# Local attention in a four-stage kernel: another written order of its steps

## The chip, the core and the metric

The kernel runs on one core of a Trainium2 chip. TensorE (PE) multiplies matrices, and loads its weights beside that (PEld); VectorE (DVE), ScalarE (ACT) and GpSimd (POOL) compute elementwise and reduce; SyncE (SP) issues DMAs. Each engine works through its own instructions in the order in which they were written and waits for the others by semaphores. The metric is the device time of one execution in microseconds (us), shown as the median of several runs. The profile comes from one further execution.

## The reference

The program has four stages over 16 sequences of 256 tokens and 128 features: a full attention, a transformer of six layers with local attention, a state space model and a small feed-forward layer. The change lies in the second stage, which computes this for each layer (shortened):

```python
qkv = x @ Wqkv                                  # 16 heads of 64
q, k = l2norm(q) * qs, l2norm(k) * ksc
q = q * cos * scale + rotate_half(q) * sin * scale
k = k * cos * inv + rotate_half(k) * sin * inv
sim = einsum('bhwie,bhwje->bhwij', bq, bk2) * 8  # windows of 32, look back one window
attn = softmax(where(mask, -max, sim), -1)
x = einsum('bhwij,bhwje->bhwie', attn, bv2) @ Wo + x
x = (a * gelu(gate)) @ W2 + b2 + x               # a, gate from the normalized x
```

Before both halves of a layer, half of the features are shifted by one token (shift_tokens).

## The kernel before

Everything is float32. In the transformer the 16 sequences form 8 groups of two, so that six layers give 48 groups. A group's work is cut into named steps, each of which is a method of the class Transformer. In a step's name, q or k says which of the two is made, the first digit is the sequence in the group (b), the second the half of 128 tokens (t), and a third, where there is one, a half of the data.

PE's steps are P (L613, projection of q or k, two matmuls of 512 columns), T (L687, 16 transposes of 64 rows), X (L714, two transposes of the input), S (L744, 64 small score matmuls), G (L802, eight matmuls that apply the probabilities, in four row groups of 32 side by side), Y (L823, four heads of the output projection, four Ys for each sequence), and, in the feed-forward half, F1 (L843), F5, FP (L899) and FY (L923).

DVE's steps are C and N (L629, L641, rotary products), R (L653, sums of squares), RR, MX and SB (L757, L763, maximum and its subtraction), SM (L776), TP (L790, transpose of the probabilities), FADD, F2, FM (L910) and FF. FF adds the layer's result to the state F; in the last layer it issues four instructions more. ACT's are Q (L623, squares), E (L704, copies of T's result to qT or kT), W (L717, copy of X's result), K (L731, the mask into the score tile), EX (L772, exponentials), B (L813, copies of G's result to `at`), SQ, F4, F6 and FE. POOL's are A (L660), M (L675), NR (L783), MXS, F3 and FN. V is two DMAs on SP's queue, which make the copy of W's result that is shifted by one window.

The order is written out by hand as a list of 172 steps, ORDER. The text behind the @ of a step is its lag. In period p the loop walks through the list once and issues each step for group p minus its lag, so one period interleaves steps of up to four groups:

```python
for p in range(n + last):
    ...
    if j >= NG - 2 and i + 1 < DEPTH:
        self.value_output(i + 1, j - NG + 2)
    ...
    for name, lag in steps:
        if 0 <= p - lag < n:
            self.step(name, groups[p - lag])
```

In the last two periods of the first five layers, value_output (L593, L603) makes half of the next layer's product of value and output weights, ahead of the period's first step: 8 small matmuls into a tile pw and two ACT copies out of it. In the fifth period of a layer, load fetches the next layer's weights.

PE writes to PSUM, where the steps share five tiles: three of the kind `two` (two banks each: pq of P, pt of T, s of K and S, pa of G, fp of FP, pw) and two of the kind `one`. They are handed out by a list of free ones, in the order of the program:

```python
def take(self, shape, name, uses=1):
    i = self.free.pop(0)
```

A step that takes a tile waits until the last reader of that tile's user before has finished. A pq is dropped after Q, C and N have read it, an s after SB, an fp after FE and FM. G takes two tiles of the kind `two`, each with half of the windows, and drops nothing but its input; the B steps drop them:

```python
for i in range(2):
    g.pa[b, t, i] = self.two.take([P, 2, HEADS * W], "pa")
```

Of the kernel before, what the change touches and what calls it, by code (L numbers as in the profile page):

```python
# [34 lines left out]
FF = int(D * 4 * 2 / 3)  # L35
# [423 lines left out]


ORDER = """
Pq00@0 FM2@3 Cq00@0 Nq000@0 EX01@1 Mq10@1 Mk10@1 SM01@1 EX00@1 G10@2 Qq000@0 FADD0@2 B101@2 B100@2
Ak11@1 FY@3 Nq001@0 Aq00@0 SM00@1 Qq001@0 Rq00@0 G11@2 B111@2 FF@3 Mq11@1 X0@1 Pk01@0 Ck01@0 Tk10@1
B110@2 Pq01@0 Nk010@0 Nk011@0 W0@1 Ek10@1 Qk010@0 Cq01@0 Qk011@0 Pk00@0 Ak01@0 Tq10@1 V0@1 Qk000@0
Qk001@0 Nq010@0 Nq011@0 Aq01@0 NR00@1 Y10@2 Eq10@1 Y11@2 Qq010@0 Qq011@0 Rk01@0 Rk00@0 NR01@1 Ck00@0
K10@1 Nk000@0 Rq01@0 MXS0@0 Mk11@1 Tq11@1 Eq11@1 S10@1 Nk001@0 TP00@1 Ak00@0 Pq11@0 MX10@1 SB10@1
SQ0@0 Qq110@0 Nq110@0 Nq111@0 Cq11@0 Pq10@0 Qq100@0 Qq101@0 Tk11@1 Y12@2 Qq111@0 Nq100@0 Nq101@0
Cq10@0 Ek11@1 Y13@2 FADD1@2 G00@1 K11@1 B000@1 S11@1 TP01@1 B001@1 X1@1 G01@1 RR0@0 EX10@1 Aq10@0
MX11@1 Mk00@0 SB11@1 F1@2 F2@2 B010@1 B011@1 Mq00@0 W1@1 EX11@1 Rq10@0 Mq01@0 Pk10@0 Pk11@0 Qk110@0
Tk00@0 Ek00@0 F3@2 FN@2 F4@2 Ck10@0 Nk100@0 Nk101@0 Ck11@0 Aq11@0 V1@1 Y00@1 Tq00@0 Eq00@0 Y01@1  # L470
Tq01@0 F5@2 Qk100@0 Y02@1 Qk101@0 K00@0 SM11@1 F6@2 Mk01@0 SM10@1 S00@0 Eq01@0 Tk01@0 Rk10@0 Nk110@0
Nk111@0 NR11@1 TP11@1 Qk111@0 MX00@0 SB00@0 Ek01@0 FP0@2 FE0@2 Rk11@0 K01@0 FP1@2 NR10@1 Y03@1
Rq11@0 MXS1@0 FE1@2 FM0@2 FM1@2 Ak10@0 SQ1@0 TP10@1 RR1@0 S01@0 MX01@0 FP2@2 FE2@2 SB01@0
"""


# [1106 lines left out]
```

## Time and profile before

| what | value |
|---|---|
| median of 3 runs | 3877.59 us (3875.69 to 3879.16) |
| profiled execution | 3872.05 us, its span 3870.2 us |
| first P of the transformer | 431.4 us after the span's start |
| last FF | ends at 3321.3 us, with its four last additions at 3323.3 us |
| mean granted TensorE clock | 0.985 |

The first 430 us of the span are the full attention, the stretch to 3323 us is the transformer, and the rest are the other two stages. From one group's F1 to the next group's there are 47 distances, of which the last two, at the end, are shorter because steps of earlier lags have run out.

A row of the page's section on slices has one digit for each fortieth of the span, in tenths of busy time. A row of the windows view gives the window, its length, and the busy time and number of instructions of PE, PEld, DVE, ACT and POOL, then the granted clock, the DMA share and GB/s. A row of the timeline gives start, duration, engine, line, operation, tiles written and read, shapes, number of merged instructions, and in brackets the idle time before and what ended it. A row of the waits view tells who waited for whom: us in total, times, the longest. Matmuls are pipelined and their ends are modelled, so the distance from one step's start to the next one's is what PE spends on it.

### The profile page before, as it was taken

What the parts mean: (1) busy time and instruction counts of PE and PEld (TensorE: products, weight loads), DVE (VectorE), ACT (ScalarE), POOL (GpSimd) and SP (SyncE); (2) the same over time, 40 slices, a digit from 0 to 9 for tenths busy, and PEclk for the clock granted to TensorE, in tenths of its full rate; (3) what the DMA queues carried; (4) which work ended last, traced back from release to release, by engine and by line L of the source; (5) the groups of instructions that cost most, each with busy time, mean ns of one, the idle gap of its engine ahead of it and who ended that gap; (6) DMA issues with size and microseconds to landing.
All of it is one profiled execution on the core that took longest, in us unless ns stands there. A gap on an engine that the chain in (4) does not pass through costs nothing. (4 is left out here: it accounts for less than half of the span.)

```text
span 3870.2 us, 104028 instructions
## 1 busy us (share of the span) xinstructions
PE 3691.9 (95%) x45040; PEld 2197.4 (57%) x45040; DVE 3386.8 (88%) x4736; ACT 2820.3 (73%) x4008; POOL 2604.4 (67%) x1636
## 2 busy tenths in 40 slices
PE   8999689999999999999999999999999999699997
PEld 4445355665656656655655656666566556355554
DVE  4665489999999999999999999999999998399997
ACT  3565467777777777777777777777777676589895
POOL 2222477777777777777777777777777775288887
PEclk9999799999999999999999999999999999899999
DMA  1000001000010000100001000000000000243432
GB/s 54 8 7 5 1 7 34 6 7 6 6 35 6 6 7 6 34 6 7 6 5 34 7 6 6 15 25 6 6 7 6 6 6 7 65 111 103 128 108 71
DMA packets 84166, 94.42 MB, mean 24 GB/s; under 512 B 8873, under 2 KB 55805, under 8 KB 82941
## 3 DMA queue, kind: packets, MB, share of 16 engines
q1 hardware_dynamic: 83708, 87.76, 8.3%
q8 instruction: 355, 5.82, 0.7%
q14 instruction: 103, 0.84, 0.1%
HBM read 73.84 MB, written 2.62 MB: 20 GB/s over the span
## 5 line engine op out<-in xcount | busy, mean ns | idle before, releaser
L660 POOL TENSOR_TENSOR u<-u,w 128x1024 f32<-128x1024 f32 x384 | 907.7, 2368 | 402.3 <-DVE w L641 236.7
L675 POOL TENSOR_TENSOR u<-u,r 128x1024 f32<-128x1024 f32 x384 | 725.0, 1904 | 17.6 <-DVE r L671 14.9
L823 PE MATMUL py<-at,wvo 128*128 128x256 f32 x3072 | 733.2, 387 | 3.7 <-ACT at L813 2.3
L613 PE MATMUL pq<-wqk,F 128*128 128x512 f32 x1536 | 715.3, 603 | 9.8 <-ACT sq L623 3.3
L623 ACT ACTIVATE sq<-pq 128x512 f32<-128x512 f32 x768 | 432.8, 600 | 300.1 <-PE pq L613 155.1
L823 PEld LDWEIGHTS py<-at,wvo 128*128 128x128 f32 x3072 | 566.5, 191 | 105.7 <-issue 22.5
L641 DVE TENSOR_TENSOR w<-pq,sinl 128x512 f32<-128x512 f32 x768 | 499.6, 681 | 8.9 <-ACT sq L623 2.1
L629 DVE TENSOR_TENSOR u<-pq,cosl 128x1024 f32<-128x1024 f32 x384 | 466.8, 1216 | 45.6 <-PE pq L613 42.5
L813 ACT COPY at<-pa 128x1024 f32<-128x1024 f32 x384 | 368.7, 1012 | 157.4 <-PE pa L802 157.4
L653 DVE TENSOR_REDUCE ss<-sq 128x16 f32<-128x1024 f32 x384 | 451.7, 1197 | 6.2 <-ACT sq L623 6.2
L613 PEld LDWEIGHTS pq<-wqk,F 128*128 128x128 f32 x1536 | 276.7, 191 | 296.6 <-issue 256.3
L802 PE MATMUL pa<-pT,xw 32*128 32x512 f32 x3072 | 407.0, 616 | 5.2 <-ACT sq L623 1.8
L783 POOL TENSOR_TENSOR pp<-pp,sm 128x1024 f32<-128x1024 f32 x192 | 363.7, 1915 | 32.0 <-DVE sm L779 32.0
L687 PEld LDWEIGHTS pt<-ident,u 64*128 64x128 f32 x6144 | 224.9, 140 | 228.1 <-issue 77.2
L1324 DVE TENSOR_TENSOR_SCAN s<-da,db 128x512 f32<-128x512 f32 x256 | 301.1, 1208 | 24.6 <-PE db L1318 12.7
L744 PEld LDWEIGHTS s<-kT,qT 64*32 64x32 f32 x24576 | 255.9, 105 | 88.3 <-issue 79.0
L687 PE MATMUL pt<-ident,u 64*128 64x64 f32 x6144 | 276.7, 230 | 30.4 <-ACT sq L623 10.9
L744 PE MATMUL s<-kT,qT 64*32 64x64 f32 x24576 | 288.8, 227 | 15.3 <-issue 10.4
L757 DVE TENSOR_REDUCE mx<-s 128x16 f32<-128x1024 f32 x192 | 230.4, 1200 | 66.4 <-PE s L744 64.8
L252 DVE TENSOR_REDUCE mx<-s 128x2 f32<-128x512 f32 x256 | 165.3, 687 | 139.9 <-PE sT L280 121.5
L802 PEld LDWEIGHTS pa<-pT,xw 32*128 32x128 f32 x3072 | 179.9, 185 | 170.2 <-issue 75.9
L899 PE MATMUL fp<-hT,w 128*128 128x512 f32 (+1 forms) x576 | 273.2, 611 | 0.9 <-ACT hT L884 0.9
(212 smaller groups left out, 6275.7 us busy)
## 6 DMA issues: line engine op xcount, KB each, us to landing
btd<-bc SPq DMA_DIRECT2D x72, 512.0 KB
bte<-bc SPq DMA_DIRECT2D x56, 256.0 KB
xw<-xw SPq DMA_DIRECT2D x96, 96.0 KB
wqk<-in_Wqk SPq DMA_DIRECT2D x6, 1024.0 KB
wv<-in_LWvT SPq DMA_DIRECT2D x6, 512.0 KB
wo<-in_Wo SPq DMA_DIRECT2D x6, 512.0 KB
xin<-in_x SPq DMA_DIRECT2D x8, 256.0 KB
out<-ot SPq DMA_DIRECT2D x8, 256.0 KB
```

Of the source, the lines that this page charges most:

```text
L613: nc.tensor.matmul(q.p[:, x], self.F[:, g.b0 + b, o : o + P], g.l.wqk[:, k, x, :], start=True, stop=True)
L623: self.c.nc.scalar.activation(q.sq[:, x], q.p[:, x], AF.Square)
L629: self.c.nc.vector.tensor_tensor(q.u.rearrange("p h x d -> p x h d"), q.p, g.l.cosl[:, t, k].unsqueeze(2).to_broadcast([P, 2, HEADS, DH // ...
L641: self.c.nc.vector.tensor_tensor(q.w[:, :, x], q.p[:, 1 - x], g.l.sinl[:, t, k, x, :].unsqueeze(1).to_broadcast([P, HEADS, DH // 2]), ALU. ...
L653: self.c.nc.vector.tensor_reduce(g.ss[b][:, t, k, :], q.sq.rearrange("p x h d -> p h x d"), AX.XY, ALU.add)
L660: self.c.nc.gpsimd.tensor_tensor(q.u, q.u, q.w, ALU.add)
L675: self.c.nc.gpsimd.tensor_tensor(uf, uf, g.r[b][:, t, k, :].unsqueeze(2).to_broadcast([P, HEADS, DH]), ALU.mult)
L687: self.c.nc.tensor.matmul(q.pt[:, r, j, :], uf[rs, j * P : (j + 1) * P], self.c.ident[rs, rs], is_transpose=True, start=(j == 0), stop=Tru ...
L744: nc.tensor.matmul(s[qs, e, j, :], qT[es, j, qs], kT[es, j, ks : ks + 2 * W], start=False, stop=True, skip_group_check=True,)
L802: self.c.nc.tensor.matmul(g.pa[b, t, w // 2][:, w % 2, :], self.xw[b][qs, t, k, :], g.pT[b, t][qs, k, :], start=(k == 0), stop=(k == 1),)
L813: self.c.nc.scalar.copy(self.at[:, :, o : o + 2 * W].rearrange("p h (w q) -> p w h q", q=W), g.pa[b, t, i].rearrange("p w (h q) -> p w h q ...
L823: self.c.nc.tensor.matmul(g.py[b], g.l.wvo[:, h, :], self.at[:, h, :], start=(h == 0), stop=(h == HEADS - 1),)
```

## The change

The list ORDER is replaced by another order of the same 172 steps. No step, tile, size or engine is changed. 25 steps change their lag: Tq00, Tk00, Tk01, S00, S01, with their E, K, MX and SB, and Mk01, Ak10, MXS1, SQ1 and RR1 go from lag 0 to 1; Y02, Y03, W1, V1 and TP11 from 1 to 2; FM0 from 2 to 3.

```diff
 ORDER = """
-Pq00@0 FM2@3 Cq00@0 Nq000@0 EX01@1 Mq10@1 Mk10@1 SM01@1 EX00@1 G10@2 Qq000@0 FADD0@2 B101@2 B100@2
-Ak11@1 FY@3 Nq001@0 Aq00@0 SM00@1 Qq001@0 Rq00@0 G11@2 B111@2 FF@3 Mq11@1 X0@1 Pk01@0 Ck01@0 Tk10@1
-B110@2 Pq01@0 Nk010@0 Nk011@0 W0@1 Ek10@1 Qk010@0 Cq01@0 Qk011@0 Pk00@0 Ak01@0 Tq10@1 V0@1 Qk000@0
-Qk001@0 Nq010@0 Nq011@0 Aq01@0 NR00@1 Y10@2 Eq10@1 Y11@2 Qq010@0 Qq011@0 Rk01@0 Rk00@0 NR01@1 Ck00@0
-K10@1 Nk000@0 Rq01@0 MXS0@0 Mk11@1 Tq11@1 Eq11@1 S10@1 Nk001@0 TP00@1 Ak00@0 Pq11@0 MX10@1 SB10@1
-SQ0@0 Qq110@0 Nq110@0 Nq111@0 Cq11@0 Pq10@0 Qq100@0 Qq101@0 Tk11@1 Y12@2 Qq111@0 Nq100@0 Nq101@0
-Cq10@0 Ek11@1 Y13@2 FADD1@2 G00@1 K11@1 B000@1 S11@1 TP01@1 B001@1 X1@1 G01@1 RR0@0 EX10@1 Aq10@0
-MX11@1 Mk00@0 SB11@1 F1@2 F2@2 B010@1 B011@1 Mq00@0 W1@1 EX11@1 Rq10@0 Mq01@0 Pk10@0 Pk11@0 Qk110@0
-Tk00@0 Ek00@0 F3@2 FN@2 F4@2 Ck10@0 Nk100@0 Nk101@0 Ck11@0 Aq11@0 V1@1 Y00@1 Tq00@0 Eq00@0 Y01@1
-Tq01@0 F5@2 Qk100@0 Y02@1 Qk101@0 K00@0 SM11@1 F6@2 Mk01@0 SM10@1 S00@0 Eq01@0 Tk01@0 Rk10@0 Nk110@0
-Nk111@0 NR11@1 TP11@1 Qk111@0 MX00@0 SB00@0 Ek01@0 FP0@2 FE0@2 Rk11@0 K01@0 FP1@2 NR10@1 Y03@1
-Rq11@0 MXS1@0 FE1@2 FM0@2 FM1@2 Ak10@0 SQ1@0 TP10@1 RR1@0 S01@0 MX01@0 FP2@2 FE2@2 SB01@0
+Pk01@0 FM2@3 W1@2 FM0@3 Nk010@0 Nk011@0 Tq00@1 Ck01@0 Tk00@1 FY@3 TP11@2 MXS1@1 Mk01@1 V1@2 SQ1@1
+RR1@1 Ak11@1 FF@3 Eq00@1 Tk01@1 Ak01@0 Ak10@1 Mk10@1 Mq11@1 Mk11@1 Ek00@1 Pk00@0 Qk010@0 Qk011@0
+Nk000@0 Rk01@0 K00@1 S00@1 Ek01@1 MX00@1 Pq00@0 SB00@1 Qk000@0 Qk001@0 Ck00@0 Qq000@0 Qq001@0 Cq00@0
+Nk001@0 Y02@2 Y03@2 K01@1 S01@1 Nq000@0 Nq001@0 MX01@1 SB01@1 Mq10@1 G11@2 X0@1 Ak00@0 EX00@1
+FADD0@2 Aq00@0 B111@2 B110@2 G10@2 EX01@1 Pq11@0 B100@2 B101@2 Pq01@0 SM00@1 Rk00@0 Qq110@0 Qq111@0
+SM01@1 Tk11@1 Ek11@1 Rq00@0 Nq110@0 Qq010@0 Cq11@0 Qq011@0 NR01@1 Y10@2 Nq111@0 Aq11@0 TP01@1 Tq11@1
+Eq11@1 Cq01@0 Y11@2 Tk10@1 W0@1 V0@1 Pq10@0 Y12@2 Nq010@0 Nq011@0 NR00@1 Ek10@1 K11@1 Rq01@0 MXS0@0
+Aq01@0 SQ0@0 S11@1 Tq10@1 Y13@2 Nq100@0 Cq10@0 Nq101@0 TP00@1 Qq100@0 Aq10@0 Qq101@0 MX11@1 Eq10@1
+SB11@1 EX11@1 G00@1 B001@1 B000@1 FADD1@2 Rq11@0 F1@2 RR0@0 SM11@1 Mq01@0 F2@2 NR11@1 F3@2 FN@2
+Mk00@0 Rq10@0 G01@1 B011@1 B010@1 Pk10@0 Nk100@0 Ck10@0 Pk11@0 K10@1 Qk110@0 Nk101@0 S10@1 Nk110@0
+Nk111@0 Y00@1 MX10@1 F4@2 Qk100@0 Qk101@0 F5@2 SB10@1 Tq01@0 F6@2 EX10@1 Ck11@0 Y01@1 SM10@1 Qk111@0
+Eq01@0 Rk11@0 FP1@2 FE1@2 FP2@2 FE2@2 Rk10@0 FP0@2 NR10@1 FM1@2 TP10@1 FE0@2 X1@1 Mq00@0
 """
```

## The prediction, as it was put on record

> The profiled execution took 3872.05 us, 3870.2 of it span and about 2 around it; the median of the three runs shown, 3877.59, lies 5.5 above it. I sum against the profiled execution and add the sum to the median. About 0.2% (8 us) is what a measurement of this kernel tells from no change.
>
> **What bounds the kernel now.** I read the page's busy line and slices first, then the windows of three periods of the written order (a period runs from one F1 to the next), then the waits, then the timeline at the places that the change touches.
>
> ```profile
> PE 3691.9 (95%) x45040; PEld 2197.4 (57%) x45040; DVE 3386.8 (88%) x4736; ACT 2820.3 (73%) x4008; POOL 2604.4 (67%) x1636
> PE   8999689999999999999999999999999999699997
> PEclk9999799999999999999999999999999999899999
> ```
>
> ```profile
> 918.90:977.00 58.10, 57.94 (x834) 35.30 (x830) 55.62 (x76) 44.76 (x59) 43.16 (x25) 1.00 0.03 6
> 1093.40:1153.00 59.60, 57.92 (x835) 35.11 (x831) 56.13 (x76) 44.82 (x59) 44.82 (x29) 1.00 0.18 52
> 2918.70:2978.90 60.20, 57.95 (x834) 35.28 (x830) 57.55 (x80) 44.65 (x59) 43.20 (x25) 1.00 0.02 6
> ```
>
> The columns are PE, PEld, DVE, ACT, POOL. A plain period is 58.1 us and PE idles 0.16 us of it; ACT and POOL have over 13 us to spare, DVE 2.5. The second window holds the next layer's value_output, the third is of the last layer, where FF issues four more instructions on DVE. Full clock in all three. So the layers are PE's, and an order gains or loses by what it makes PE wait.
>
> ```profile
> PEld pa L802 <- ACT at L813: 29.7, 56, 0.8
> PEld pq L613 <- ACT kT L704: 8.1, 34, 0.2
> ```
>
> Over 34 periods, G's weight loads wait for B's copies again and again, and one P per period waits 0.24 us for an E.
>
> **The G pairs, the main term.** G takes two of the three `two` tiles. Here is G10, FY, G11, and then G00, S11, X1, G01:
>
> ```profile
> 943.52 2.00 PE L802 MATMUL pa<-pT,xw 32*128 32x512 f32 x16
> 945.45 2.84 PE L923 MATMUL fy<-act,w 128*128 128x512 f32 x6
> 946.29 1.92 ACT L813 COPY at<-pa 128x1024 f32<-128x1024 f32 x2
> 948.22 0.34 PEld L802 LDWEIGHTS pa<-pT,xw 32*128 32x128 f32 x8 [0.76 <-ACT at L813]
> 948.22 2.03 PE L802 MATMUL pa<-pT,xw 32*128 32x512 f32 x16
> 950.18 0.44 PE L714 MATMUL x<-ident,F 128*128 128x128 f32 x2
> 950.46 1.45 PE L613 MATMUL pq<-wqk,F 128*128 128x512 f32 x3
> ```
>
> ```profile
> 971.12 2.25 PE L802 MATMUL pa<-pT,xw 32*128 32x512 f32 x16
> 973.15 1.93 ACT L813 COPY at<-pa 128x1024 f32<-128x1024 f32 x2 [1.57 <-PE pa L802]
> 973.30 1.48 PE L744 MATMUL s<-kT,qT 64*32 64x64 f32 x128
> 974.71 0.44 PE L714 MATMUL x<-ident,F 128*128 128x128 f32 x2
> 975.08 2.04 PE L802 MATMUL pa<-pT,xw 32*128 32x512 f32 x16
> ```
>
> In both, the second G starts in the same hundredths as the pair of copies ends (946.29 + 1.92 = 948.21; 973.15 + 1.93 = 975.08): it is held by them, and what lies between (FY 2.77 us from start to start; S11 1.41 and X1 0.37) just covers the copies. A clean G is over 2.00 us after its start and lets the next step start after 1.93.
>
> The new order puts G11, X0, G10 and G00, F1, G01: one short step where 2.77 and 1.78 us lay. The other step's tile is now free, so the second G needs one copy, not two: its first tile is the third slot, its second tile the one that the first B drops. From the first G's start that tile is free at 2.00 + 0.04 (hand-over) + 1.01 (one copy) = 3.05. PE arrives at 1.93 + 0.37 = 2.30 behind X0 and at 1.93 + 0.58 = 2.51 behind F1 (0.49 to a P, 1153.00 to 1153.49 below; 0.09 more to a G, as X shows: 0.28 at 950.18, 0.37 at 974.71). PE loses 0.75 + 0.54 = 1.29 us. That half of the second G can start early saves nothing: the G at 971.12 has two of its four row groups 0.26 late and lasts 2.25 for 2.00, and the next step comes 2.18 behind it.
>
> ```profile
> 1153.00 0.65 PE L843 MATMUL f<-ident,F 128*128 128x128 f32 x4
> 1153.49 0.59 PE L613 MATMUL pq<-wqk,F 128*128 128x512 f32 x1
> ```
>
> Over 45 full periods: +58. Bounds: 0, if ACT hands over earlier than either row has it; +100, if B is late besides, for EX11 stands directly ahead of B001 in ACT's new queue and EX00 ahead of B111 (1.06 us each, and they wait for SB on DVE).
>
> [...]
>
> **Waits that go.** The P that waits for kT now has other neighbours: -0.24 x 45 = -11. The late half of G00 (0.25) waits for a DVE read of a `pq` tile; G11 in the new order takes its second tile in the same way, so between 0 and -11, I take -5.
>
> **PE's own work.** The same matmuls. One transpose step now follows another (Tq00, Tk00), while Y10, Y11 and Y00, Y01 are split by T; both are changes of tile shape of 0.1 us or so, as F1's and X's exits show. Net 0, between -5 and +5.
>
> **Periods with value_output** (ten; two at the end of each of five layers):
>
> ```profile
> 1234.09 1.16 PE L593 MATMUL pw<-wo,wv 64*128 64x128 f32 x16
> 1235.18 1.98 PE L613 MATMUL pq<-wqk,F 128*128 128x512 f32 x4
> 1235.30 1.07 ACT L603 COPY wvo<-pw 128x512 f32<-128x512 f32 x2 [0.42 <-PE pw L593]
> ```
>
> Now P follows pw after 1.09 us. In the new order FM2 and FM0 are written behind the period's first P, so two of three `two` tiles are still held there; pw gets the last one and Pk01 must take it back after both copies: 1235.30 + 1.07 - 1234.09 = 2.28. 2.28 - 1.09 = 1.19, x 10 = +12, bounds 0 and +20.
>
> **The last layer.** Its periods are 60.2, 2.1 over a plain one, because FF's four extra instructions (57.55 against 55.62 us on DVE) catch up with PE. A PE that is 1 us slower per period leaves DVE that much more room: -1.0 x 5 = -5, bounds -10 and 0.
>
> **Fill and drain.** MX00, SB00, MX01, SB01 go from a group's own period to the next, Y02, Y03, TP11 and FM0 likewise: some 5 us of DVE work (four at 1.2) leave the first period and come back behind the last. I take 0; bounds -8 and +12, the drain being a chain.
>
> **At no cost.** Exp, Sqrt and Gelu now change places five times per period for six, one ACT_TABLE_LOAD of 1.28 us less; ACT's 13 us of spare time hide that, as they would hide its return. POOL's A, M and NR are moved within 43 of 58 us. V1's two DMAs move behind W1@2 in SP's queue, which holds little else; ten PE steps, over 15 us, lie before the G that reads them.
>
> **Sum:** 58 - 11 - 5 + 0 + 12 - 5 + 0 = +49: 3921 for the profiled execution, 3927 on the median. Its own range is 3900 to 3950.
>
> **Rivals.** *Faster:* the copies do not hold PE, because the tile is ready when X0 or F1 ends. Then the P and G waits (0.49 x 45 = 22) and most of the last layer's loss (2.1 x 5 = 10) go, with 5 from the fill: -37, 3840. It decides where the tile is free within 2.30 and 2.51 us of the first G's start; both rows put one copy at 3.05, which speaks against it. For it speaks that B has 13 us of idle ACT around it. *No change:* later steps now wait anyway for DVE (2.5 us of slack), so a stall at G swallows others: about +3, 3880. Against it: no listed wait but those above reaches PE. *Slower still:* SB11 comes late, EX11 holds ACT's queue, B001 waits behind it, and G01 behind that: one EX, 1 us more per period, +94, 3971.
>
> **How the numbers follow.** Main case 0.72, slower still 0.13, no change 0.06, faster 0.09. The range from 3869 to 3963 leaves out the faster case and the upper part of the slowest. Chances: slower 0.84 (the main case with all but a corner of its range, and the slower one), same 0.06, faster 0.10.
>
> **What would show it.** In the profile after: F1 to F1 near 59.0 instead of 58.1; the second G of each pair about 3.05 us behind the first, with PEld waiting for ACT `at`; value_output periods near 61; ACT_TABLE_LOADs fewer by about 45. I am wrong if second Gs start 2.3 to 2.5 us behind the first, or if plain periods stay at 58.1 or fall to 57.5.

## The result, and the profile after

The changed kernel takes 3971.84 us (median of four runs, 3970.51 to 3976.19) against 3878.38 (3875.69 to 3881.32) before: a ratio of 1.0243, interval 1.0225 to 1.026. The profiled span is 3969.0 us against 3870.2. The direction is the predicted one and the size is double: +93 instead of +49, and outside the range.

The page of the kernel after, its busy line and slices:

```profile
PE 3757.0 (95%) x45040; PEld 2237.7 (56%) x45040; DVE 3453.0 (87%) x4736; ACT 2766.8 (70%) x3962; POOL 2604.7 (66%) x1636
...
PE   8999699999999999999999999999998989699997
...
PEclk9999799999999999999999999999999999799999
```

No engine has more instructions than before, and ACT has 46 fewer, the table loads that were to go. Yet PE is busy for 65 us more and DVE for 66. PE's slices fall below 9 in two places near the end of the transformer that were full before (8 and 8 around a 9). The windows of a plain period, one with value_output and one of the last layer, as in the prediction (PE, PEld, DVE, ACT, POOL, clock, DMA share, GB/s), in the kernel after:

```profile
921.40:980.60 59.20, 59.04 (x835) 36.13 (x831) 56.41 (x76) 43.63 (x57) 43.14 (x24) 1.00 0.02 6
1217.60:1279.30 61.70, 60.37 (x851) 37.12 (x847) 56.49 (x76) 44.70 (x59) 43.12 (x24) 1.00 0.02 6
3030.30:3098.10 67.80, 61.84 (x834) 37.02 (x830) 64.25 (x80) 43.59 (x57) 43.75 (x24) 0.95 0.02 5
```

The first two are what was predicted (59.0 and 61). The third was to be near 60 and is 67.8. There PE idles for 6 us, the mean granted clock is 0.95, and DVE's 80 instructions take 64.25 us instead of 57.55. Cut at the F1s, the two spans compare so (us):

| part of the span | before | after | difference | predicted |
|---|---|---|---|---|
| up to the first P | 431.4 | 428.8 | -2.6 | } 0 with the drain |
| first P to first F1 | 134.5 | 126.6 | -7.9 | } |
| 30 plain periods | 1755.2 | 1791.0 | +35.8 | +28 |
| ten with value_output | 597.6 | 616.5 | +18.9 | +21 |
| five of the last layer | 303.5 | 339.6 | **+36.1** | **0** |
| drain (to the last L945) | 101.1 | 119.4 | +18.3 | } |
| the rest | 546.9 | 547.1 | +0.2 | 0 |

The column of predictions takes the recorded terms by period: (58 - 11 - 5) / 45 = 0.93 for each, 1.19 more with value_output, 1.0 less in the last layer. Waits of PE over the transformer after (total, times, longest):

```profile
PE s L744 <- ACT s L731: 29.8, 5, 6.0
PE pq L613 <- ACT wvo L603: 11.7, 10, 1.2
PE pt L687 <- issue: 8.2, 3, 4.0
PE pa L802 <- DVE pp L763: 5.8, 35, 0.4
PE py L823 <- issue: 2.6, 1, 2.6
```

The first line is new: five waits of 6 us, one in each period of the last layer. The second is the predicted wait behind value_output, 1.17 us each for 1.19. The third and the fifth belong to three slow plain periods, to which I come back, and the fourth is a wait of a G for DVE.

**The last layer.** The timeline of one of its periods in the kernel after, from the additions on (all engines; lines between left out):

```profile
3053.34 4.68 POOL L660 TENSOR_TENSOR u<-u,w 128x1024 f32<-128x1024 f32 x2
...
3056.57 7.86 DVE L945 SCALAR_TENSOR_TENSOR xT<-F,m0mod,xT 64x256 f32<-64x256 f32 x4
...
3058.10 8.09 POOL L675 TENSOR_TENSOR u<-u,r 128x1024 f32<-128x1024 f32 x4
...
3064.46 0.69 DVE L641 TENSOR_TENSOR w<-pq,sinl 128x512 f32<-128x512 f32 x1
...
3065.25 2.06 ACT L623 ACTIVATE sq<-pq 128x512 f32<-128x512 f32 x4 [9.07 <-DVE w L641]
3066.20 1.21 DVE L757 TENSOR_REDUCE mx<-s 128x16 f32<-128x1024 f32 x1
3067.45 1.23 DVE L763 TENSOR_TENSOR pp<-s,mx 128x1024 f32<-128x1024 f32 x1
...
3068.70 1.02 ACT L731 COPY s<-mask 128x1024 f32<-128x1024 f32 x1 [1.39 <-DVE pp L763]
...
3069.77 2.06 PE L744 MATMUL s<-kT,qT 64*32 64x64 f32 x128 [5.96 <-ACT s L731]
```

Read it backwards from PE's wait: S waits for K, K for the `two` tile that SB (L763) gives back, SB for MX, MX for N and R ahead of it on DVE, and all of them for four additions that take 7.86 us. POOL is busy with A and M during all of them. The same line's durations (minimum, median, maximum, in ns), first after, then before:

```profile
L945 DVE SCALAR_TENSOR_TENSOR xT<-F,m0mod,xT x32: 476/2007/2015, 2989.2 to 3421.4; 64x256 f32<-64x256 f32 x32
```

```profile
L945 DVE SCALAR_TENSOR_TENSOR xT<-F,m0mod,xT x32: 475/484/2119, 2952.5 to 3322.8; 64x256 f32<-64x256 f32 x32
```

The operation goes from a median of 0.484 us to 2.007 with the same operands. The trace of before had two slow ones out of 32 (2.119 and 2.015 us), both in the drain, one beside an L783 on POOL and one beside an L675; everywhere else POOL was idle under them.

**The G pairs.** PE's timeline in the kernel after: F1 and G01 (G00 is just ahead of them); then G11, X0, G10:

```profile
921.44 0.66 PE L843 MATMUL f<-ident,F 128*128 128x128 f32 x4
922.02 2.60 PE L802 MATMUL pa<-pT,xw 32*128 32x512 f32 x16
924.55 3.70 PE L613 MATMUL pq<-wqk,F 128*128 128x512 f32 x8
...
956.30 2.28 PE L802 MATMUL pa<-pT,xw 32*128 32x512 f32 x16
958.51 0.44 PE L714 MATMUL x<-ident,F 128*128 128x128 f32 x2
959.11 2.57 PE L802 MATMUL pa<-pT,xw 32*128 32x512 f32 x16 [0.16 <-DVE pp L763]
961.61 3.70 PE L613 MATMUL pq<-wqk,F 128*128 128x512 f32 x8
```

From start to start G01 takes 924.55 - 922.02 = 2.53 us and G10 2.50, where a clean G takes 1.93: losses of 0.60 and 0.57. They lie inside the second G: two of its row groups start when PE arrives and the others when the copy is done, as the weight loads of G01 show:

```profile
922.02 0.30 PEld L802 LDWEIGHTS pa<-pT,xw 32*128 32x128 f32 x4 [0.17 <-issue]
922.64 0.73 PEld L802 LDWEIGHTS pa<-pT,xw 32*128 32x128 f32 x10 [0.32 <-ACT at L813]
```

### The profile page after: what moved, and what is told of

Read it like the earlier page. It is cut to its first block, busy times and chain, and to the rows that moved or that the text cites. A ratio compares the mean times of both kernels' runs of the same rounds, so it can differ in the third digit from the quotient of the medians.

```text
span 3969.0 us, 104215 instructions
## 1 busy us (share of the span) xinstructions
PE 3757.0 (95%) x45040; PEld 2237.7 (56%) x45040; DVE 3453.0 (87%) x4736; ACT 2766.8 (70%) x3962; POOL 2604.7 (66%) x1636
## 5 line engine op out<-in xcount | busy, mean ns | idle before, releaser
L660 POOL TENSOR_TENSOR u<-u,w 128x1024 f32<-128x1024 f32 x384 | 901.4, 2363 | 194.1 <-DVE w L641 160.5
L675 POOL TENSOR_TENSOR u<-u,r 128x1024 f32<-128x1024 f32 x384 | 728.0, 1912 | 187.7 <-DVE r L671 184.0
L613 PE MATMUL pq<-wqk,F 128*128 128x512 f32 x1536 | 739.6, 615 | 17.0 <-ACT wvo L603 11.7
L823 PE MATMUL py<-at,wvo 128*128 128x256 f32 x3072 | 746.9, 389 | 4.3 <-issue 2.6
L783 POOL TENSOR_TENSOR pp<-pp,sm 128x1024 f32<-128x1024 f32 x192 | 367.3, 1913 | 466.0 <-ACT qT L704 313.7
L623 ACT ACTIVATE sq<-pq 128x512 f32<-128x512 f32 x768 | 422.7, 600 | 296.8 <-DVE w L641 166.7
L641 DVE TENSOR_TENSOR w<-pq,sinl 128x512 f32<-128x512 f32 x768 | 499.9, 681 | 131.9 <-PE pq L613 119.4
L802 PE MATMUL pa<-pT,xw 32*128 32x512 f32 x3072 | 471.1, 629 | 12.8 <-DVE pp L763 9.0
L629 DVE TENSOR_TENSOR u<-pq,cosl 128x1024 f32<-128x1024 f32 x384 | 461.2, 1211 | 20.0 <-PE pt L687 19.8
L744 PE MATMUL s<-kT,qT 64*32 64x64 f32 x24576 | 288.8, 228 | 36.0 <-ACT s L731 35.8
L1324 DVE TENSOR_TENSOR_SCAN s<-da,db 128x512 f32<-128x512 f32 x256 | 301.0, 1207 | 24.7 <-PE db L1318 10.0
L802 PEld LDWEIGHTS pa<-pT,xw 32*128 32x128 f32 x3072 | 211.8, 189 | 151.0 <-issue 96.3
L687 PE MATMUL pt<-ident,u 64*128 64x64 f32 x6144 | 267.6, 230 | 24.7 <-POOL u L675 11.5
L704 ACT COPY kT<-pt 128x1024 f32<-128x1024 f32 x192 | 194.4, 1012 | 120.6 <-PE pt L687 120.6
L1334 PE MATMUL y<-hc,ident 128*128 128x512 f32 x512 | 244.3, 604 | 16.0 <-POOL hc L1328 14.2
```

The lines of the kernel that those rows point to most:

```text
L613: nc.tensor.matmul(q.p[:, x], self.F[:, g.b0 + b, o : o + P], g.l.wqk[:, k, x, :], start=True, stop=True)
L623: self.c.nc.scalar.activation(q.sq[:, x], q.p[:, x], AF.Square)
L629: self.c.nc.vector.tensor_tensor(q.u.rearrange("p h x d -> p x h d"), q.p, g.l.cosl[:, t, k].unsqueeze(2).to_broadcast([P, 2, HEADS, DH // ...
L641: self.c.nc.vector.tensor_tensor(q.w[:, :, x], q.p[:, 1 - x], g.l.sinl[:, t, k, x, :].unsqueeze(1).to_broadcast([P, HEADS, DH // 2]), ALU. ...
L660: self.c.nc.gpsimd.tensor_tensor(q.u, q.u, q.w, ALU.add)
L675: self.c.nc.gpsimd.tensor_tensor(uf, uf, g.r[b][:, t, k, :].unsqueeze(2).to_broadcast([P, HEADS, DH]), ALU.mult)
```

## The experiments

Two theories were to be told apart from their rivals. *Additions:* the last layer's 36 us come from L945 meeting POOL's A and M. *Copies:* the 1 us of a plain period comes from a second G that comes before the first one's copies are done. In all but the third, fifth and last three, the starting point is the kernel after or the first experiment.

**1. The additions where POOL idles.** The kernel after, with the four additions as a step of their own:

```diff
-MX10@1 F4@2 Qk100@0 Qk101@0 F5@2 SB10@1 Tq01@0 F6@2
+MX10@1 F4@2 Qk100@0 Qk101@0 F5@2 SB10@1 FG@3 Tq01@0 F6@2
...
+    def FG(self, g):
+        nc = self.c.nc
         if g.layer == DEPTH - 1:
```

> The new order, with the last layer's four additions to xT (L945) taken out of FF and issued as a step of their own behind SB10, where POOL is idle (8 to 14.8 us behind F1 in the new order's profile). Theory (POOL beside L945 makes it slow): L945 falls from 2.01 to 0.48 us, the last layer's periods from 67.4 to 68.2 to about 60 (59.1 plus what 1.9 us more DVE work costs), plain periods stay at 59.1; total about 3972 - 38 to -45 = 3927 to 3934, ratio to the kernel before near 1.013. Rival (the four additions cost 2 us each because of where they stand among DVE's own steps or because of what they read, whatever POOL does): L945 stays near 2 us and the time within 5 us of 3972.

Measured: 3930.34 us (3928.89 to 3933.16), ratio to before 1.0137 (1.0122 to 1.0152). The additions' line in this kernel (moved to L949 by the edit):

```profile
L949 DVE SCALAR_TENSOR_TENSOR xT<-F,m0mod,xT x32: 466/480/485, 3037.9 to 3380.7; 64x256 f32<-64x256 f32 x32
```

None is slow. (In one group of the drain the additions met a POOL instruction of another size, L53 on 128x4, and here POOL's was the one that grew, from 1.04 us to 1.25; the additions, of which the first had started 0.09 us earlier, kept their 0.48.) The five periods take 301.0 us instead of 339.6, the drain 113.3 instead of 119.4, and plain (59.13) and value_output periods (61.65) stay as they were. So 41.5 of the 93 us are the additions. What is left, +52, is near what the prediction had worked out for everything else (+49 with the last layer's -5, so +54 without), in part by luck: terms that had been taken as 0 came to something and nearly cancelled, as shown below.

**2. The additions with one operand fewer.** The kernel after; L945 becomes a product without the sum with the old xT (that sum is left out):

```diff
-nc.vector.scalar_tensor_tensor(xb, src, self.m[p, 5, bi : bi + 1], xb, ALU.mult, ALU.add)
+nc.vector.tensor_scalar(xb, src, self.m[p, 5, bi : bi + 1], None, ALU.mult)
```

> The new order, L945 in its place, but with one tensor operand: the scaled F is written over xT and the sum with what xT held before is left out, so the residual of the last layer is missing. Theory as narrowed (what slows L945 beside POOL is that it reads two tensors from SBUF; L936, the same operation with one of them in PSUM, takes 0.48 beside POOL in the same periods): 0.3 to 0.5 us each, last layer's periods near 60. If any DVE work that touches SBUF alone is slowed by POOL: near 2 us each again, periods stay at 67 to 68.

Measured: 3970.8 us (one run), the last five periods 336.5.

```profile
L945 DVE TENSOR_SCALAR xT<-F,m0mod x32: 344/1872/1951, 2992.6 to 3421.5; 64x256 f32<-64x256 f32 x32
```

Alone the product takes 0.344 us, beside POOL 1.87 at the median. My narrower theory, that two operands in SBUF are what matters, fell: one suffices in this form. The order of events in the two traces tells more. In the kernel after, POOL's instructions end at 3058.02, 3060.07, 3062.11 and 3064.15, and the four additions at 3058.30, 3060.35, 3062.39 and 3064.43, each 0.28 us behind; meanwhile POOL's M goes from 1.90 us to 2.08. Each of the 24 additions there that started beside an L660 or L675 ended 0.27 or 0.28 us behind the end of POOL's instruction, so I read most of the 2.01 us that their records show at the median as waiting. How it waits is not shown: an addition that did nothing before POOL's instruction had ended should, by its 0.48 us alone, end some 0.48 us behind it, not 0.28. L936, the instruction just ahead (the same operation and shape, with one operand in PSUM), takes 0.47 to 0.49 beside the same L660.

**3. The converse.** The kernel before, with the additions moved behind Rk00, where POOL works:

```diff
-Rk01@0 Rk00@0 NR01@1 Ck00@0
+Rk01@0 Rk00@0 FG@3 NR01@1 Ck00@0
```

> The order of before, with L945 taken out of FF and issued behind Rk00, where POOL works without a break (A, A, NR, NR at 38 to 47 us behind F1). Theory: L945 rises from 0.48 to about 2.0 us, the last layer's periods from 60.2 to 65 or more, total about +25 to +35. Rival (place among DVE's steps in the new order alone): L945 stays at 0.48 and the time within 5 us of before.

Measured: 3891.64 us (one run) against 3878.11; the last five periods 63.5 to 65.3 us instead of 60.2 to 61.4.

```profile
L949 DVE SCALAR_TENSOR_TENSOR xT<-F,m0mod,xT x32: 475/624/2115, 2962.3 to 3343.1; 64x256 f32<-64x256 f32 x32
```

In each of the five periods three of the four met POOL: two took 2.0 us, one that started just before the end of POOL's instruction 0.63, and the last 0.48. The sign and the mechanism are the theory's; +13.5 instead of 25 to 35, because POOL's work did not last for all four.

**4. FY between the G pair.** The kernel after, with FY in X0's place, X0 behind G10, and FADD0 and FF moved along:

```diff
-Mq10@1 G11@2 X0@1 Ak00@0 EX00@1 FADD0@2 Aq00@0 B111@2 B110@2 G10@2 EX01@1
+FADD0@2 Mq10@1 G11@2 FY@3 Ak00@0 EX00@1 Aq00@0 B111@2 B110@2 G10@2 X0@1 EX01@1
```

> The new order with FY instead of X0 between G11 and G10, X0 behind G10, FADD0 ahead of both and FF behind SM00. FY (2.77 us from start to start) covers one copy. Theory (the second G waits for the first one's copy): the wait of 0.5 to 0.75 us at G10 goes, plain periods from 59.13 to 58.4 to 58.6. Rival (PE waits for DVE there anyway): plain periods stay at 59.1. The last layer's L945 move with FF, so the total tells less than the periods; by periods alone 3972 - 25 = 3947.

Measured: 3933.03 us, ratio 1.0141 (1.0124 to 1.0158). But the plain period is still 59.13. PE's timeline in this kernel, the Ts that FY stood between before, and then the G pair:

```profile
943.45 1.21 PE L688 MATMUL pt<-ident,u 64*128 64x64 f32 x32
945.36 0.72 PE L688 MATMUL pt<-ident,u 64*128 64x64 f32 x16 [0.70 <-ACT qT L705]
946.18 1.98 PE L614 MATMUL pq<-wqk,F 128*128 128x512 f32 x4
948.25 1.48 PE L745 MATMUL s<-kT,qT 64*32 64x64 f32 x128
...
956.45 2.13 PE L803 MATMUL pa<-pT,xw 32*128 32x512 f32 x16
958.51 2.84 PE L924 MATMUL fy<-act,w 128*128 128x512 f32 x6
961.28 2.00 PE L803 MATMUL pa<-pT,xw 32*128 32x512 f32 x16
963.21 0.44 PE L715 MATMUL x<-ident,F 128*128 128x128 f32 x2
```

The pair is healed: the second G takes 1.93 and X 0.28. But Tq00, Tk00 and Tk01 now follow one another, three takers of three `two` tiles, and wait for E's copies: from 943.45 to 946.18 is 2.73 us, where T and T (1.15) and T (0.65) took 1.80 around FY in the kernel after. A loss of 0.93 returned there. FY had been their cover. G11 and X gained besides (0.15 and 0.32) and the P behind the Ts lost 0.16; that gains and losses cancel to 0.01 us of a period is chance or the sign of another chain that sets it, and no run here separates the two. The total fell by 39 us all the same because FF moved with FY, to a place where POOL all but idles (additions 0.48 us, the last five periods 299.6): the first experiment's gain by another way.

**5. A short step between the pair in the kernel before.** FADD0 and FY go ahead of G10, so G10 and G11 are neighbours:

```diff
-SM01@1 EX00@1 G10@2 Qq000@0 FADD0@2 B101@2 B100@2 Ak11@1 FY@3 Nq001@0
+SM01@1 EX00@1 FADD0@2 FY@3 G10@2 Qq000@0 B101@2 B100@2 Ak11@1 Nq001@0
```

> The order of before with FY (and FADD0 ahead of it) moved in front of G10, so that nothing lies between G10 and G11. Theory (the second G waits until the first one's tiles are copied out, and FY was the cover): G11 starts 3.0 to 4.0 us behind G10 instead of 1.93, plain periods go from 58.13 to 59.2 to 60.2, total +45 to +90. Rival (the time would come back elsewhere, because some other loop sets the period): plain periods within 0.3 of 58.13.

Measured: 3954.96 us (one run) against 3879.12; the plain period goes from 58.13 to 59.95.

```profile
957.39 2.00 PE L803 MATMUL pa<-pT,xw 32*128 32x512 f32 x16
960.52 2.90 PE L803 MATMUL pa<-pT,xw 32*128 32x512 f32 x16 [1.13 <-ACT at L814]
963.35 0.44 PE L715 MATMUL x<-ident,F 128*128 128x128 f32 x2
```

The second G starts 3.13 us behind the first (3.05 in the prediction's working) and takes 2.83; the pair takes 5.96 us where it took 3.89. One uncovered pair costs 2.07, of which 1.82 stays in the period.

**6. value_output written later.** The first experiment's kernel, with value_output issued behind FM0 instead of ahead of the period's first step:

```diff
-            if j >= NG - 2 and i + 1 < DEPTH:
-                self.value_output(i + 1, j - NG + 2)
...
                     self.step(name, groups[p - lag])
+                if name == "FM0" and j >= NG - 2 and i + 1 < DEPTH:
+                    self.value_output(i + 1, j - NG + 2)
```

> The new order with L945 as its own step behind SB10 (as in the first experiment, 3930) and value_output issued behind FM0 instead of ahead of Pk01, so that pw takes a tile that FM2 has given back and Pk01 has one of its own. Theory (Pk01 waits for both copies of pw): periods with value_output fall from 61.65 to 59.9 to 60.6, total -10 to -17. Rival (the extra 2.5 us are the work of value_output itself): 61.65 stays.

Measured: 3925.51 us (3923.03 to 3930.44), ratio 1.0118 (1.0102 to 1.0133); the ten periods go from 61.65 to 60.97. From pw to the next step PE now takes 0.99 us instead of 2.33, so the reading of the tiles was right; but the T behind it takes 1.98 instead of 1.14 and gives 0.84 of the 1.34 back. The X and the P ahead of them are 0.19 shorter together. The 0.68 gained are less than expected.

**7. The layer's weights in three parts.** The first experiment's kernel, with load spread over three periods:

```diff
-            if j == last + 1 and i + 1 < DEPTH:
-                self.load(i + 1)
+            if j in (last, last + 1, last + 2) and i + 1 < DEPTH:
+                self.load(i + 1, j - last)
```

> The new order with L945 as its own step (3930), and a layer's weights loaded in three parts, in three periods instead of one (2.87 MB in some 11 us before). Theory (the 5 us that PE loses in three periods come because PE's instructions are fetched over the same DMA engines behind the weights): periods of 64.8, 64.5 and 63.5 fall below 61, total -8 to -14. Rival (these three waits have nothing to do with the load): they stay.

Measured: 3930.11 us, ratio 1.0131 (1.0112 to 1.015). The three slow plain periods fell from 64.8, 64.5 and 63.5 us to 63.9, 63.4 and 60.7, but three others rose to 60.4, 60.8 and 62.7; together the plain periods lose 18.8 us over their median instead of 17.8. PE's stalls for "issue" (4.04, 3.84 and 2.55 us in the kernel after) lie in the stretch in which the weights arrive, but spreading them did not take the loss away. The DMA records of the traces show what goes ahead of these stalls. One queue of the kind "instruction" (q8) brings 354 packets of 16 KB in the kernel after, one for every 256 of the 90,791 records of PE, its sequencer and PEld. Each of PE's stalls for "issue" over 0.5 us in the transformer, eight in the kernel before and three in the kernel after, ends 1.25 to 1.60 us behind the landing of such a packet; at a moment taken at random one would have landed so in 1 case of 26 (295 landings between 555 and 3302 us in the kernel after, so one in 9.3 us, and a stretch of 0.35 us). That PE had run out of instructions there is how I read these records. That the weights held the three packets back, as the theory had it, is argued and not shown: of the eight stalls before, 0.74 to 1.69 us long, five come where the DMA share is 0.01.

**8. Half the copies.** The first experiment's kernel, in which each B copies 8 of 16 heads (the other heads' part of the output is left out):

```diff
-            self.at[:, :, o : o + 2 * W].rearrange("p h (w q) -> p w h q", q=W),
-            g.pa[b, t, i].rearrange("p w (h q) -> p w h q", q=W),
+            self.at[:, 0:PAIRS, o : o + 2 * W].rearrange("p h (w q) -> p w h q", q=W),
+            g.pa[b, t, i].rearrange("p w (h q) -> p w h q", q=W)[:, :, 0:PAIRS, :],
```

> The new order with L945 as its own step (3930), and every B copies only 8 of the 16 heads (the other half of `at` stays zero, so half of the heads are missing from the output). A copy takes some 0.5 us instead of 1.0. Theory (PE waits for B at the G pairs): G01's and G10's waits of 0.6 and 0.8 us shrink by 0.5 each, plain periods from 59.13 to 58.1 to 58.4. Rival, left standing by the run with FY between the Gs (some other loop sets 59.13): 59.0 to 59.1.

Measured: 3885.79 us (one run); the plain period is 58.28 instead of 59.13.

```profile
948.86 2.29 PE L804 MATMUL pa<-pT,xw 32*128 32x512 f32 x16
951.08 0.44 PE L716 MATMUL x<-ident,F 128*128 128x128 f32 x2
951.67 2.15 PE L804 MATMUL pa<-pT,xw 32*128 32x512 f32 x16 [0.15 <-DVE pp L765]
953.75 3.70 PE L615 MATMUL pq<-wqk,F 128*128 128x512 f32 x8
```

The second Gs go from 2.50 and 2.53 to 2.08 and 2.11 (the other pair): the copies were what they waited for, but for 0.15 and 0.18 us that stay. The first G of the pair (2.22) and X (0.59) did not move, so their losses of 0.28 and 0.22 (against 1.93 and 0.37) are not the copies'; the wait that the trace shows there is for DVE.

**9. The same in the kernel before**, as a control for the eighth:

> Control for the half copies: the kernel before, in which every B copies 8 of 16 heads (the other half of the heads' outputs is left out). Theory: in the kernel before, FY, S11 and X1 cover the copies, all but 0.28 us at G10/G11 and 0.25 at the late half of G00, so plain periods fall by 0 to 0.5 us (57.6 to 58.1), against 0.85 in the kernel after. Rival (half copies save PE time by something other than the wait for the tile): plain periods fall by 0.85 here too, to 57.3 or below.

Measured: 3878.09 us (one run) against 3879.16; the plain period is 58.13, as without the edit. Half copies gain nothing where FY, S11 and X1 cover them, and 0.85 us a period where X0 and F1 stand.

**10. Before, with the additions on ACT and POOL**, a try at a kernel better than both: four ACT instructions scale F, one POOL instruction per sequence adds.

```diff
-                    nc.vector.scalar_tensor_tensor(
-                        xb, src, self.m[p, 5, bi : bi + 1], xb, ALU.mult, ALU.add
-                    )
+                    nc.scalar.activation(y[p], src, AF.Identity, scale=self.m[p, 5, bi : bi + 1])
+                xb = self.c.xT[:, bi * S : (bi + 1) * S]
+                nc.gpsimd.tensor_tensor(xb, xb, y, ALU.add)
```

> The kernel before, with the four additions of the last layer (L945) taken off DVE: four ACT instructions scale F by m into a new tile, one POOL instruction adds that to xT, behind X0. Theory (in the kernel before, what sets the last layer's periods is DVE, whose 57.55 us hold those additions): the last layer's five periods go from 60.2 to 61.4 us down to 58.1 to 58.6, the total falls by 8 to 14 us, to about 3866. Rival (those periods are long for another reason, X or the loads): they stay at 60.2 and over, total within 3 us of before. Second rival (POOL's addition slows DVE's instructions beside it, as DVE and POOL slowed each other in the kernel after): single DVE instructions of 1 us or more over their usual time show up in the last layer, and the periods keep at least 1 us of the 2.1.

Measured: 3882.69 us against 3879.16, ratio 1.0008 (0.9998 to 1.0017). The five periods fell from 303.5 to 299.1 us, four of them to 59.5 or 59.6 but not to 58, and the drain grew by 9 us. PE's waits in four periods of the last layer in this kernel:

```profile
PE pq L614 <- ACT at L814: 5.6, 4, 1.4
```

DVE is no longer late, and no instruction of DVE got longer; ACT's four scalings stand ahead of B110 in its queue, and a P waits 1.4 us for that copy. Neither the theory nor a rival had this.

**11. Before, with the additions on POOL alone**, behind Mq11, for all but the last two groups:

```diff
+                        nc.gpsimd.tensor_scalar(y[p], src, self.m[p, 5, bi : bi + 1], None, ALU.mult)
...
+                    nc.gpsimd.tensor_tensor(xb, xb, y, ALU.add)
```

> The kernel before, with the last layer's four additions (L945) taken off DVE for all but its last two groups, onto POOL alone (four products of F and m, two additions to xT), behind Mq11, where POOL waits 4.7 us for DVE; ACT gets nothing. Theory: in the kernel before, the additions' 2 us on DVE delay the next C and N, and so Q and the T behind it (a gap of 1.84 us at a T in the period at 3040); with ACT's four scalings in their place the T was free, but B110 was late, and a P waited 1.4 us. Without both, the five periods of the last layer come to 58.1 to 58.8 us (four of the five hold such groups, and the fifth too), the drain keeps its 101, and the total falls by 6 to 11 us. Rival (the wait at the T has another cause, which the scalings hid): the periods stay at 59.5 or over, total within 4 us of before. Second rival (POOL's products slow DVE's C and N beside them): DVE's instructions behind FF take longer than 1.21 and 0.68 us, and the periods keep 1 us or more of the 2.1.

Measured: 3882.61 us against 3882.39, ratio 1.0 (0.999 to 1.001); the periods are 60.3.

```profile
L956 POOL TENSOR_SCALAR fg<-F,m0mod x24: 916/924/928, 2955.3 to 3257.5; 64x256 f32<-64x256 f32 x24
```

Four products of 0.92 us and two additions of 0.73 fill 5.4 us, more than POOL's gap of 4.7; the next A ends late, and an N on DVE waits 1.93 us for it. The T that had waited 1.84 us now follows without a gap, as the theory said; later steps wait instead. Over a plain period those of the last layer are 2.1 to 3.3 us long with the additions on DVE, 2.2 to 2.5 on POOL, and 1.4 (once 2.9) on ACT and POOL, and neither version ran faster than the kernel before.

## Why the prediction was wrong, by its own steps

**The last layer: the step that failed.** The prediction took FF's four additions as four instructions of 0.48 us and asked only whether DVE had room for them (-1.0 x 5 = -5, bounds -10 and 0; it took the five periods for 60.2 us long, and two of them are 61.4). Measured: +36.1 in the five periods and, by the first experiment, 6.1 more in the drain (119.4 - 113.3). What moved was not DVE's load but what runs beside it: in the new list FF stands ahead of Ak01, Ak10, Mk10, Mq11 and Mk11, a long stretch of POOL's work. The additions took 1.73 + 3 x 2.01 = 7.76 us instead of 1.92. Those 5.8 us go whole through SB, a tile and K to S (6.0 of PE idle). S itself then takes 1.99 us from start to start instead of 1.41 and the G behind it is slow as well, where the granted clock is 0.50 (3069 to 3071 us) and 0.62 (3071 to 3077), against 0.95 over the period. The prediction put "POOL's A, M and NR are moved" among the edits at no cost, judging by POOL's own spare time. It should have asked which DVE instructions come to lie beside them. The trace of before held the price, 2.119 us as the maximum of L945. With the additions at 0.48 (first experiment) the five periods are 301.0 us, 2.5 less than before. In excess over a plain period that is 5.4 us in all instead of 12.8, so the direction of the -5 holds; but the additions also stand elsewhere there, and what each of the two did is not separated.

**The G pairs: right.** 1.29 us a period were worked out; 0.60 behind F1 (0.54 predicted) was measured. At G10 0.57 lie in the G itself and the X ahead of it loses 0.22, which by the eighth experiment is not the copies' (0.75 predicted, all of it for the copy). My sign for it was badly chosen: G01 starts 2.51 us behind G00, which I had named as what would prove me wrong, and G10 2.81 behind G11, neither of them 3.05, because half of the second G can start when PE arrives. I had said that this saves nothing, and the length (2.53 instead of 1.93) shows it. G11 is itself 0.28 long, in the place of the 0.25 that G00 lost before, so nothing came of the -5; the P's wait of 0.24 for kT did go. Plain periods rose by 1.00 with 0.93 predicted: the main term is shown, but that the sum is so close is in part luck, with a loss at X that no term held. The eighth and ninth experiments show the copies as the cause. PEld is busy for 36.13 of the 59.20 us of a plain period after, and the second Gs wait all the same.

**Periods with value_output: right.** 2.11 us more at the median (61.65 - 59.54), 2.12 predicted (1.89 in the mean, since before had one of 61.15); 1.24 at pw's exit for 1.19. The sixth experiment confirms which tile it was.

**Fill, drain and start:** the fill gained 7.9 and the start 2.6, and the drain, without its additions' 6.1, lost 12.2: together +1.7 for a predicted 0. That is luck: fill and drain each missed by 8 to 12 us and nearly cancelled, and the start lies in a stage that was not changed (it is 428.8 to 436.8 in the runs here).

**What no term held:** three plain periods that are 4.3 to 5.9 us longer than the others, at PE stalls for "issue". The kernel before loses 11.4 us over its median in plain periods and the kernel after 17.0, so 5.6 us of the difference lie here. The stalls over 0.5 us come to 10.4 us in either kernel, eight short ones before and three long ones after. Each ends 1.25 to 1.60 us behind the landing of an instruction packet (seventh experiment); why they gathered into three and then cost more is not settled.

**The rivals.** *Faster* fell with the measured lengths of the second Gs. *No change* fell with the 1.00 us of a plain period, and in the fifth experiment too only 0.25 of the 2.07 us was made up elsewhere. *Slower still* gave 3971, which is the measured time, by chance, for a reason that is not there: plain periods would have been 60.1 and are 59.13.

## What to carry to other kernels

When an order is rewritten, list for each moved elementwise step of VectorE what GpSimd will run beside it, and take the maximum of its row in the trace, not only the mean: here L945's maximum of 2.119 us, at a median of 0.484, showed what it costs in bad company. Look twice at busy time that grows at the same instruction count: here L945's median went from 0.484 to 2.007 us, and I read most of that as waiting. And a long step between two takers of the same few tiles can cover waits where it stands: here, with three tiles, moving FY took 0.57 us off G10 and lost 0.93 at the Ts (fourth experiment). So cost the place that it leaves too.

## What the runs showed of the hardware that I had not expected

A DVE addition of 64x256 f32 with both operands in SBUF took 0.48 us alone and 2.01 beside POOL's L675 of 1.9 us, and a product with one operand 0.344 and 1.87 (second experiment); the additions ended 0.27 or 0.28 us behind the POOL instruction that they met. POOL's own (L675) grew by 0.18 us at most. Beside POOL's L53 of 128x4 the addition kept its 0.48 us and POOL's grew by 0.21 (first experiment). The same operation with one operand in PSUM (L936) kept its 0.48 us beside L660, and DVE's products from PSUM (L629, L641) kept their 1.21 and 0.68 us, in the kernel after beside POOL's L660 and L675 and in the eleventh experiment beside its 0.92 us products. PE's stalls for "issue" over 0.5 us each ended 1.25 to 1.60 us behind the landing of a 16 KB instruction packet, and the longest took 4.04 us.
